# Deformable convolution: three accumulating joins per tile instead of four, with ScalarE weighting one neighbour into PSUM

## The chip, the cores and the metric

The kernel runs on one core of a Trainium2 chip as a single program. The metric is the time of one execution on the device in microseconds (us), and lower is better. Six executions of the kernel before lie between 6318.02 and 6331.94 us, with a median of 6324.73 us. The profile is that of one further execution.

## The reference

The reference is a network of four layers, each with a convolution part and a feed-forward part on a float32 image batch `x` of shape 4 x 128 x 64 x 64 (batch, channels, rows, columns). Only the second convolution part is touched here. It is a modulated deformable 3 x 3 convolution, cut to what matters:

```python
off  = conv2d(x, w_off, b_off).reshape(B, 9, 2, H, W)   # a shift per tap and pixel
mask = sigmoid(conv2d(x, w_mod, b_mod))
py, px = row + ky + dy, column + kx + dx                # where tap k looks
y0, x0 = floor(py), floor(px); wy, wx = py - y0, px - x0
sampled = v00*(1-wy)*(1-wx) + v01*(1-wy)*wx + v10*wy*(1-wx) + v11*wy*wx
sampled = sampled * mask
out = einsum('bckhw,ock->bohw', sampled, weight) + bias
```

For every pixel and each of the nine taps, four neighbouring pixels (all 128 channels) are read at a place that depends on the data, each is multiplied by a weight of its own, and the four are added. The sum then goes through a 128 x 128 matrix per tap, and the nine results are added.

## The kernel before

The whole batch stays in on-chip memory (SBUF) as `xs`, with channels on the 128 partitions. Seven phases follow each other. The second one, `recurrence_and_deformable`, ends with `deformable`, which is the stage of this document.

**Tiling.** There are four batch images. An image has 4096 pixels, in eight chunks of 512, and a chunk has four tiles of 128 pixels. Seven of the nine taps (`BY_ASK`) are sampled by gathering; the other two (`HATS`) are computed without a gather, by the generator `hats`. A step of the main loop handles one gathered tap and two tiles of a chunk, so a chunk has 7 x 2 = 14 steps, an image 112, and the stage 448.

**One step.** `taken` (L964) takes a buffer `g` out of a ring of eight (`GATHERED`), and issues two indirect DMAs on GpSimd's queue (L969), one per tile. Each brings, for each of 128 pixels, the four neighbours with 128 channels each, from a table in device memory. Then one VectorE multiplication (L977) weights all 2 x 4 x 128 values per partition, in place. The weights come from `near_w`, a copy of this chunk's weights in PSUM (the memory that TensorE accumulates in).

**The joins.** `joined` (L980) turns pixels back to channels and adds the four neighbours in one go: for each of the two tiles, four transposing matmuls against the identity (L986) accumulate into the same 128 columns of a PSUM bank `pt`. A step so has eight such matmuls. Two steps fill a bank. ScalarE copies the bank to SBUF (`turn_back`, L1092), and TensorE multiplies the copy by the tap's matrix into `po` (`convolve`, L1099), which sums over the taps. `finish` (L1107, VectorE) adds a chunk's result to `xs`.

**The order.** The order of TensorE, ScalarE, VectorE and GpSimd is the written one (`manual_schedule`); each engine runs its instructions in that order and stops at the first one that must wait. `step` (L1109) runs what earlier steps have put off: the joins of a step are issued one step after its gathers, the copy of a full bank two steps after its last join, and the tap's matmul two steps after that. Then `step` advances `side`, the preparation of the next image (`plan`: normalisation, the offset convolution, the table, the weights), and `hats` of this chunk. There is no preparation beside the last image.

**The two taps without gathering.** `hats` (L1007) has 14 parts, one per step: a transposition of small pieces into `pr` and a copy of it by ScalarE (L1046); for each of two taps a matmul into `by` (L1011) and two ScalarE functions on it (L1017, L1020); then six parts, in each of which VectorE multiplies a fresh `by` into a square (L1025, `weighted`) and, three parts later, TensorE accumulates four small matmuls from it (L1033, `sampled`). The matmul into `by` is issued one part ahead of the multiplication that reads it. The last four parts also prepare four tiles of later chunks: a matmul into `pf` (L1001) and a scaled copy by ScalarE (L1005), in `fold`. At the start of an image five `fold` stand in a row.

**PSUM.** There are eight banks: two for `pt`, one for `po` (`out`), one each for the preparation's `pd` and `pv`, one for `near_w`, and two with the tag `by`, which `pr`, `by` and `pf` share in turn.

**Keeping the weights.** At the end of `plan`, two DMAs on SyncE's queue (L955, L958) store the indices and weights of an image for a fallback that is not run on these inputs.

Of the kernel before, what the change touches and what calls it, by code (L numbers as in the profile page):

```python
# [17 lines left out]
F32 = mybir.dt.float32  # L18
# [10 lines left out]
P = 128  # L29
# [655 lines left out]
def deformable(net, sampling):  # L685
# [11 lines left out]
    Q4 = 4  # L697
    HATS, PICKED = sampling.HATS, sampling.PICKED
    NH, H0 = len(HATS), HATS[0]
    BY_ASK = [k for k in range(KK) if k not in HATS]  # L700
    BANKS = {"pt": 2, "out": 1, "pd": 1, "pv": 1, "by": 2}
    GATHERED = 8
    tables, woff, boff = sampling.tables, sampling.woff, sampling.boff
    wk, bias, grids = sampling.wk, sampling.bias, sampling.grids
    with ExitStack() as ctx:
# [173 lines left out]
        def places(b, off):  # L879
# [73 lines left out]
            made[b] = (tables[b].rearrange("y x a b c -> (y x) (a b c)"), idx, w, pieces, turns[b])  # L953
            yield
            nc.sync.dma_start(  # L955
# [5 lines left out]

        near_w = ps.tile([P, 2, Q4, KK, 4], F32, name="dcn_near_w", bufs=1)

        def taken(rows, idx, c, k, i):  # L964


            g = sb.tile([P, 2, 4 * P], F32, name="dcn_g", tag="g", bufs=GATHERED)
            for t in range(2):
                nc.gpsimd.indirect_dma_start(  # L969
                    out=g[:, t, :],  # L970
                    out_offset=None,
                    in_=rows,
                    in_offset=bass.IndirectOffsetOnAxis(ap=idx[:, Q4 * c + i + t, k : k + 1], axis=0),
                )
            near = g.rearrange("p t (q c) -> p t q c", c=P)
            by = near_w[:, c % 2, i : i + 2, k, :].unsqueeze(3).to_broadcast([P, 2, 4, P])
            nc.vector.tensor_mul(near, near, by)  # L977
            return near

        def joined(pt, i, near):  # L980

            if i == 0:
                pt[0] = ps.tile([P, CH], F32, name="dcn_pt", tag="pt", bufs=BANKS["pt"])
            for t in range(2):
                for q in range(4):
                    nc.tensor.matmul(  # L986
                        pt[0][:, (i + t) * P : (i + t + 1) * P],
                        near[:, t, q, :],
                        net.ident,
                        is_transpose=True,  # L990
                        start=i + t + q == 0,
                        stop=i + t + q == 6,
                        skip_group_check=True,
                    )
# [12 lines left out]
        def hats(b, c, po, pieces, turned):  # L1007
# [46 lines left out]
            bent(1)  # L1054
            bys.append(picked(sampling.lines[:, 0, 0, :]))
            yield
            for m, (k, p) in enumerate(todo):
                weighted(k, p)
                if m + 1 < len(todo):
                    k1, p1 = todo[m + 1]  # L1060
                    bys.append(picked(sampling.lines[:, k1, p1, :]))
                if m >= 3:
                    sampled(*todo[m - 3])
                yield
            ahead = [t for t in range(Q4 * c + 5, Q4 * c + 9) if t < NT]
            for m in range(3, 6):
                sampled(*todo[m])
                if ahead:
                    fold(b, ahead.pop(0), turned)
                yield  # L1070
            if ahead:
                fold(b, ahead.pop(0), turned)
            yield

        with tc.manual_schedule(engines=ORDERED):
# [44 lines left out]
            for b in range(B):  # L1120
# [10 lines left out]
                for c in range(NCH):  # L1131
                    nc.vector.tensor_copy(near_w[:, c % 2], w[:, Q4 * c : Q4 * c + Q4])
                    po = {}
                    busy.append(hats(b, c, po, pieces, turned))
                    if b == 0 and c < B:
                        nc.sync.dma_start(sampling.kept[c].rearrange("c p t -> p c t"), as_chunks(net.xs[:, c, :]))
                    for k in BY_ASK:
                        pt = {}
                        for i in range(0, 4, 2):
                            at(2, joined, pt, i, taken(rows, idx, c, k, i))  # L1140
                            if i:
# [1441 lines left out]
```

## Time and profile before

| what | value |
| --- | --- |
| median of six executions | 6324.73 us (6318.02 to 6331.94) |
| the profiled execution | 6331.66 us |
| its span, first to last instruction | 6329.8 us |
| mean granted TensorE clock | 0.958 |
| TensorE (PE) busy | 5794.9 us, 92% of the span |
| VectorE (DVE) busy | 4352.0 us, 69% |
| ScalarE (ACT) busy | 3404.9 us, 54% |
| GpSimd (POOL) busy | 2066.4 us, 33% |
| stage: first gather to last join | 1318.6 to 2659.9 us |
| gathers L969 | 896, 949 ns each |
| weighting L977 | 448, 1214 ns each |
| joins L986 | 3584 |

A row of a group reads: line, engine, operation, output<-inputs, sizes, count | busy us, mean ns of one | idle time of the engine just before these instructions, and what ended it. "issue" is waiting for nothing that the profile shows. PE is TensorE's matmul side and PEld its loading of weights, which overlaps with it. Starts of matmuls are recorded, but their ends are modelled, so the distance from start to start says more than a duration. A row of the timeline reads: start, duration, engine, line, operation, names, count, and in brackets the idle time before it with what ended it. In a table of windows the clock that the throttle granted to TensorE stands behind the busy times.

### The profile page before, as it was taken

The numbers are of one execution on the slowest core, as the hardware profiler recorded it, in microseconds if no ns is written. First come the engines' busy times: TensorE is split into PE (matmuls) and PEld (weight loads), VectorE is DVE, ScalarE is ACT, GpSimd is POOL, SyncE is SP. The second block draws the span as 40 slices with busy tenths as digits, with TensorE's granted clock in tenths as the row PEclk, the third lists the DMA queues.
The fourth block names the chain that finished last, engine by engine and source line by source line (L and its number), as shares of the span: only waits on it lengthen the run. The fifth ranks groups of instructions, "written<-read, shape, count | busy, mean of one in ns | idle before, by whom it ended". The sixth has DMA issues, their size and how long they took to land. (4 is left out here: it accounts for less than half of the span.)

```text
span 6329.8 us, 97956 instructions
## 1 busy us (share of the span) xinstructions
PE 5794.9 (92%) x39923; PEld 2293.1 (36%) x39923; DVE 4352.0 (69%) x4707; ACT 3404.9 (54%) x4256; POOL 2066.4 (33%) x2015
## 2 busy tenths in 40 slices
PE   8999999879898887788988999999999999999799
PEld 2222222446566666533333222222222222222233
DVE  6888887445656564446545778777777778887666
ACT  4444443322222222251154888888888888999521
POOL 4888984046666666500000111111111111111000
PEclk9999999989999999889989999999999999999899
DMA  6443340177676776651164566656665666666300
GB/s 212 87 94 82 75 94 20 47 185 217 197 212 192 207 206 183 181 190 49 41 218 144 124 144 143 137 124 140 141 140 123 141 143 138 130 130 130 76 24 27
DMA packets 291041, 836.40 MB, mean 132 GB/s; under 512 B 43356, under 2 KB 117596, under 8 KB 244492
## 3 DMA queue, kind: packets, MB, share of 16 engines
q0 software_dynamic: 109568, 505.75, 33.9%
q1 hardware_dynamic: 181004, 324.17, 17.8%
q8 instruction: 321, 5.26, 0.3%
q14 instruction: 148, 1.21, 0.1%
HBM read 416.71 MB, written 111.10 MB: 83 GB/s over the span
## 5 line engine op out<-in xcount | busy, mean ns | idle before, releaser
L1989 ACT ACTIVATE att_ex<-att_sc,att_shift 128x1024 f32<-128x1024 f32 x2048 | 2155.6, 1111 | 330.8 <-PE att_sc L1985 150.5
L2020 DVE TENSOR_TENSOR att_dve<-att_dve,att_ex 128x2048 f32<-128x2048 f32 x704 | 1634.2, 2321 | 351.1 <-ACT att_ex L1989 328.2
L1985 PE MATMUL att_sc<-att_q,att_k 32*128 32x512 f32 x8192 | 1286.5, 646 | 16.3 <-ACT att_ex L1989 16.3
L2001 PE MATMUL att_pv<-att_ex,att_vals 128*32 128x512 f32 x8192 | 1099.2, 608 | 6.6 <-ACT att_hidden L2027 5.6
L969 POOL DMA_INDIRECT dcn_g<-dcn_table,dcn_idx x896 | 850.3, 949 | 558.6 <-issue 208.0
L412 DVE SCALAR_TENSOR_TENSOR inv_prod<-inv_pk,bspan,inv_seen 128x512 f32<-128x512 f32 (+1 forms) x1120 | 774.6, 743 | 141.5 <-PE inv_pk L399 141.2
L410 POOL TENSOR_TENSOR inv_prod<-inv_seen,inv_prod 128x512 f32<-128x512 f32 (+1 forms) x672 | 837.6, 1274 | 95.4 <-ACT inv_prod L409 95.4
L2018 POOL DMA_DIRECT2D att_dma<-att_ex x224 | 192.5, 860 | 1916.7 <-ACT att_ex L1989 1669.8
L409 ACT ACTIVATE inv_prod<-inv_pk,bspan 128x512 f32<-128x512 f32 (+1 forms) x672 | 436.1, 682 | 505.1 <-PE inv_pk L399 494.0
L1985 PEld LDWEIGHTS att_sc<-att_q,att_k 32*128 32x128 f32 x8192 | 423.5, 184 | 663.8 <-issue 437.9
L977 DVE TENSOR_TENSOR dcn_g<-dcn_g,dcn_near_w 128x1024 f32<-128x1024 f32 x448 | 533.0, 1214 | 56.9 <-DMA dcn_g<-dcn_table,dcn_idx 53.2
L986 PE MATMUL dcn_pt<-ident,dcn_g 128*128 128x128 f32 x3584 | 504.1, 286 | 69.5 <-issue 28.9
L986 PEld LDWEIGHTS dcn_pt<-ident,dcn_g 128*128 128x128 f32 x3584 | 442.6, 148 | 257.6 <-issue 188.0
L399 PE MATMUL inv_pk<-inv_red,wtap 32*96 32x512 f32 (+1 forms) x3584 | 512.2, 637 | 7.3 <-DVE wtap L377 7.3
L421 PE MATMUL inv_out<-inv_prod,inv_fold 96*32 96x512 f32 (+1 forms) x3584 | 478.5, 605 | 8.5 <-DVE xs L429 8.5
L2001 PEld LDWEIGHTS att_pv<-att_ex,att_vals 128*32 128x32 f32 x8192 | 161.8, 108 | 796.6 <-issue 760.2
L1025 DVE TENSOR_TENSOR dcn_square<-dcn_hx,dcn_by 128x512 f32<-128x512 f32 x192 | 131.1, 683 | 372.7 <-remote 97.9
L1092 ACT COPY dcn_st<-dcn_pt 128x512 f32<-128x512 f32 x224 | 129.5, 579 | 372.1 <-remote 153.3
L399 PEld LDWEIGHTS inv_pk<-inv_red,wtap 32*96 32x96 f32 (+1 forms) x3584 | 131.8, 170 | 386.7 <-DVE inv_prod L412 362.7
L1099 PE MATMUL dcn_out<-dcn_st,dcn_wk 128*128 128x512 f32 x448 | 253.6, 650 | 14.2 <-issue 6.1
L1005 ACT ACTIVATE dcn_fold<-dcn_pf,dcn_turn 128x256 f32<-128x256 f32 x128 | 60.0, 473 | 354.1 <-PE dcn_pf L1001 154.6
L1033 PE MATMUL dcn_out<-dcn_square,dcn_fold 128*128 128x128 f32 x1504 | 220.1, 288 | 16.9 <-issue 15.7
(433 smaller groups left out, 5443.5 us busy)
## 6 DMA issues: line engine op xcount, KB each, us to landing
att_dma<-att_ex POOLq DMA_DIRECT2D x224, 1024.0 KB
inv_seen<-inv_image SPq DMA_DIRECT2D x256, 266.0 KB
moe_w<-in_L_ffn_weight SPq DMA_DIRECT2D x64, 1024.0 KB
dcn_table<-dcn_xt SPq DMA_DIRECT2D x64, 512.0 KB
att_dma<-att_ex SPq DMA_DIRECT2D x32, 1024.0 KB
att_dve<-att_dma POOLq DMA_DIRECT2D x32, 1024.0 KB
moe_table<-moe_xt SPq DMA_DIRECT2D x64, 288.0 KB
dcn_g<-dcn_table,dcn_idx POOLq DMA_INDIRECT x896
```

The costliest lines, as they stand in the source:

```text
L399: nc.tensor.matmul(pk[0:m], wtap[half][rg, i, blk], red[rg, h * CH : (h + 1) * CH], start=True, stop=True)
L409: nc.scalar.activation(prod[0:m, h], pk[0:m], AF.Identity, bias=by)
L410: nc.gpsimd.tensor_mul(of, view, of)
L412: nc.vector.scalar_tensor_tensor(out=of, in0=as_shape(pk[0:m], of), scalar=by, in1=view, op0=ALU.add, op1=ALU.mult)
L421: nc.tensor.matmul(po[CR * blk : CR * (blk + 1), h, :], fold[0:m], prod[0:m, h, :], start=unit == 0, stop=unit == UNITS - 1,)
L969: nc.gpsimd.indirect_dma_start(out=g[:, t, :], out_offset=None, in_=rows, in_offset=bass.IndirectOffsetOnAxis(ap=idx[:, Q4 * c + i + t, k ...
L977: nc.vector.tensor_mul(near, near, by)
L986: nc.tensor.matmul(pt[0][:, (i + t) * P : (i + t + 1) * P], near[:, t, q, :], net.ident, is_transpose=True, start=i + t + q == 0, stop=i + ...
L1985: nc.tensor.matmul(pes[h // 2][:, h % 2, :], ks[r, t * P : (t + 1) * P], q[r], start=True, stop=True)
L1989: nc.scalar.activation(ex[:, 2 * two : 2 * two + 2, :], pes[two], AF.Exp, bias=shifts[g][:, two : two + 1],)
L2001: nc.tensor.matmul(block["pv"][r], vals[:, t, r], ex[:, h, :], start=t == 0, stop=t == NT - 1)
L2020: nc.vector.tensor_add(block[who], block[who], ex)
```

## The change

In `taken`, the multiplication by VectorE leaves the first neighbour out: it covers 2 x 3 x 128 values instead of 2 x 4 x 128. The first neighbour is weighted by ScalarE, with one instruction per tile, into a new PSUM tile `first`. VectorE then adds `first` to the second neighbour. `joined` transposes and accumulates only neighbours 1 to 3, so a step has six such matmuls.

`first` takes a PSUM bank. It comes from the tag `by`, which has one bank instead of two. `hats` is rewritten for that: the matmul into `by` is issued in the same part as the multiplication that reads it, the accumulation from a square comes two parts later instead of three, and the last four parts each do one `fold`. The DMAs that keep the weights are issued while the third chunk of the image itself is sampled, instead of at the end of its preparation.

```diff
-    BANKS = {"pt": 2, "out": 1, "pd": 1, "pv": 1, "by": 2}
+    BANKS = {"pt": 2, "out": 1, "pd": 1, "pv": 1, "by": 1}
...
             made[b] = (tables[b].rearrange("y x a b c -> (y x) (a b c)"), idx, w, pieces, turns[b])
-            yield
+
+        def keep(b, idx, w):
+
             nc.sync.dma_start(
                 sampling.all_idx[b].rearrange("c p j -> p c j"), idx.rearrange("p (c t) k -> p c (t k)", c=NCH)
             )
...
         near_w = ps.tile([P, 2, Q4, KK, 4], F32, name="dcn_near_w", bufs=1)
+        first = ps.tile([P, 2, P], F32, name="dcn_first", bufs=1)
...
-            by = near_w[:, c % 2, i : i + 2, k, :].unsqueeze(3).to_broadcast([P, 2, 4, P])
-            nc.vector.tensor_mul(near, near, by)
+            for t in range(2):
+                nc.scalar.activation(
+                    first[:, t, :], near[:, t, 0, :], AF.Copy, scale=w[:, Q4 * c + i + t, k, 0:1]
+                )
+            by = near_w[:, c % 2, i : i + 2, k, 1:].unsqueeze(3).to_broadcast([P, 2, 3, P])
+            nc.vector.tensor_mul(near[:, :, 1:], near[:, :, 1:], by)
+            nc.vector.tensor_add(near[:, :, 1], near[:, :, 1], first)
             return near
...
-                for q in range(4):
+                for q in range(1, 4):
...
-                        start=i + t + q == 0,
+                        start=i + t + q == 1,
                         stop=i + t + q == 6,
...
-            bys.append(picked(sampling.lines[:, 0, 0, :]))
             yield
             for m, (k, p) in enumerate(todo):
+                bys.append(picked(sampling.lines[:, k, p, :]))
                 weighted(k, p)
-                if m + 1 < len(todo):
-                    k1, p1 = todo[m + 1]
-                    bys.append(picked(sampling.lines[:, k1, p1, :]))
-                if m >= 3:
-                    sampled(*todo[m - 3])
+                if m >= 2:
+                    sampled(*todo[m - 2])
                 yield
             ahead = [t for t in range(Q4 * c + 5, Q4 * c + 9) if t < NT]
-            for m in range(3, 6):
-                sampled(*todo[m])
+            for m in range(4, 8):
+                if m < len(todo):
+                    sampled(*todo[m])
                 if ahead:
                     fold(b, ahead.pop(0), turned)
                 yield
-            if ahead:
-                fold(b, ahead.pop(0), turned)
-            yield
...
                     busy.append(hats(b, c, po, pieces, turned))
+                    if c == 2:
+                        keep(b, idx, w)
...
-                            at(2, joined, pt, i, taken(rows, idx, c, k, i))
+                            at(2, joined, pt, i, taken(rows, idx, w, c, k, i))
```

More of the change, by code (lines that the diff above doesn't have):

```diff
@@ L962, in deformable, with taken @@
         near_w = ps.tile([P, 2, Q4, KK, 4], F32, name="dcn_near_w", bufs=1)
-        def taken(rows, idx, c, k, i):
+        first = ps.tile([P, 2, P], F32, name="dcn_first", bufs=1)
+        def taken(rows, idx, w, c, k, i):
             g = sb.tile([P, 2, 4 * P], F32, name="dcn_g", tag="g", bufs=GATHERED)
```

## The prediction, made before the changed kernel was run

> **What bounds the kernel now.** Only the stage around `taken` changes, so I read that stage alone: first the page's groups for its costs, then a table of windows for its pace, then the timeline for what a step waits for. The chain that ended last lies in the last phase and says nothing here.
>
> From the page of the kernel before, the groups that are edited, and those that share a resource with them:
>
> ```profile
> L969 POOL DMA_INDIRECT dcn_g<-dcn_table,dcn_idx x896 | 850.3, 949 | 558.6 <-issue 208.0
> ...
> L977 DVE TENSOR_TENSOR dcn_g<-dcn_g,dcn_near_w 128x1024 f32<-128x1024 f32 x448 | 533.0, 1214 | 56.9 <-DMA dcn_g<-dcn_table,dcn_idx 53.2
> L986 PE MATMUL dcn_pt<-ident,dcn_g 128*128 128x128 f32 x3584 | 504.1, 286 | 69.5 <-issue 28.9
> L986 PEld LDWEIGHTS dcn_pt<-ident,dcn_g 128*128 128x128 f32 x3584 | 442.6, 148 | 257.6 <-issue 188.0
> ...
> L1025 DVE TENSOR_TENSOR dcn_square<-dcn_hx,dcn_by 128x512 f32<-128x512 f32 x192 | 131.1, 683 | 372.7 <-remote 97.9
> ...
> L1005 ACT ACTIVATE dcn_fold<-dcn_pf,dcn_turn 128x256 f32<-128x256 f32 x128 | 60.0, 473 | 354.1 <-PE dcn_pf L1001 154.6
> ```
>
> The joins are TensorE's largest group of the stage. The other two rows to notice are the last: VectorE sits idle 372.7 us before 192 multiplications of `hats`, and ScalarE 354.1 us before 128 copies of `fold`. Both wait for TensorE.
>
> The windows of the stage, first counting the joins alone, then all work; one window for each image:
>
> ```profile
> core 0: us, PE busy (x) PEld busy (x), PEclk, DMA share, GB/s
> ...
> 2008.00:2341.00 333.00, 121.27 (x894) 106.58 (x895) 0.94 0.70 203
> 2341.00:2625.00 284.00, 116.19 (x789) 101.21 (x786) 0.90 0.64 181
> ```
>
> ```profile
> core 0: us, PE busy (x) PEld busy (x) DVE busy (x) ACT busy (x) POOL busy (x), PEclk, DMA share, GB/s
> ...
> 2008.00:2341.00 333.00, 288.62 (x1812) 207.83 (x1812) 203.63 (x250) 90.08 (x168) 210.83 (x224) 0.94 0.70 203
> 2341.00:2625.00 284.00, 227.37 (x1361) 175.21 (x1358) 147.20 (x154) 60.45 (x110) 183.91 (x195) 0.90 0.64 181
> ```
>
> A chunk has 112 joins, so the third image takes 333 / (894/112) = 41.7 us per chunk and the last, with no preparation beside it, 284 / (789/112) = 40.3. PE is busy 36.2 and 32.3 us of these. So 3.9 us less PE work in a chunk made it only 1.4 us shorter, a share of 0.36. PE is the busiest engine by far, but its work alone does not set the pace.
>
> From the timeline, a stretch in which PE waits for nothing, and one in which others wait for it:
>
> ```profile
> 1905.47 1.04 PE L986 MATMUL dcn_pt<-ident,dcn_g 128*128 128x128 f32 x8
> ...
> 1906.35 1.06 PE L1033 MATMUL dcn_out<-dcn_square,dcn_fold 128*128 128x128 f32 x8
> ```
>
> ```profile
> 2426.34 0.38 PE L1011 MATMUL dcn_by<-dcn_rowt,dcn_lines 128*128 128x512 bf16 x1
> ...
> 2429.86 0.38 PE L1011 MATMUL dcn_by<-dcn_rowt,dcn_lines 128*128 128x512 bf16 x1 [1.41 <-ACT dcn_hx L1017]
> ...
> 2432.79 0.69 DVE L1025 TENSOR_TENSOR dcn_square<-dcn_hx,dcn_by 128x512 f32<-128x512 f32 x1 [11.79 <-PE dcn_pt L986]
> ...
> 2435.68 0.95 POOL L969 DMA_INDIRECT dcn_g<-dcn_table,dcn_idx  x1 [0.30 <-issue]
> 2436.93 0.94 POOL L969 DMA_INDIRECT dcn_g<-dcn_table,dcn_idx  x1 [0.30 <-issue]
> ```
>
> Eight joins follow each other in 0.88 us, 0.11 us each. The `by` begun at 2426.34 was read only at 2432.79, by an engine idle for 11.79 us: TensorE's results reach their readers up to some 6 us after the modelled end. And gathers can't come closer than 1.25 us.
>
> **The change part by part.** All sums are made against the profiled execution: span 6329.8 us, 6331.66 us with what lies around it, 6.9 us above the median of 6324.73.
>
> *Joins removed.* 448 steps x 2 = 896 matmuls with their loads. The low price of one is its distance in the dense stretch, 0.11 us: 99 us. The high one is the mean load, 148 ns: 133 us. Since the results arrive late, PE's true pace is slower than its recorded starts; I take 133. What of it shortens the stage lies between the share 0.36 (48 us) and all (133 us). I take 0.36, since it was measured on this loop: **-48 us**.
>
> *VectorE.* From 1024 elements in 1214 ns (L977) and 512 in 683 ns (L1025, which also reads PSUM) an element costs 1.04 ns and an instruction 152 ns. The shorter multiplication is 949 ns, the added addition of 256 elements 418 ns: 1.37 us per step instead of 1.21, 69 us in all. It lies beside PE: in the third image VectorE is busy 203.63 of 333 us, and this makes it some 220. If the cover is gone, it costs up to 69 us, in the parts where VectorE has a square to make too (0.95 + 0.42 + 0.69 = 2.06 us against a step of 41.7 / 14 = 2.98).
>
> *ScalarE.* 896 new instructions of 128 elements. Below stands the 64x128 copy L802 at 298 ns, above L1005 with its scale at 473 ns. I take 350: 314 us, 0.70 us per step. ScalarE is busy 90.08 of 333 us, and will be about 170. That is hidden by PE as well. But these instructions wait for the gather and, since `first` is a single tile, for the addition of the step before. Behind them in ScalarE's order stand the copies of `pt` (L1092), of `pr`, and of `fold`, and TensorE waits for all of these. The circle addition, two weightings, addition takes 0.42 + 0.70 us and two hand-overs of some 0.05 (in the timeline PE starts 0.05 us after the ScalarE function that it waited for), 1.2 us against 2.98. So I cost it at nothing; the cover is the eight buffers, a step's data lying ready before it is wanted. The gather frees its buffer later only where the joins do.
>
> *One bank for `by`.* Per chunk eleven uses now wait for the reader of the use before: the second of the first two matmuls, six multiplications, four `fold`, less the first that had to wait anyway. Between two uses PE has six joins (0.66 us), half a tap's matmul and, in most parts, four small ones (0.88 us); the reader needs 0.47 to 0.69 us and two hand-overs. Low end: nothing. High end: the whole reader exposed, 0.8 us x 11 x 32 = 282 us. By the table of PE's waits in the stage it waits today 12.2 us for squares, 5.1 for the functions and 6.3 for `fold` at these places, 23.6 us with two banks. The value is nearer to this low row than to the high end, and I add half as much again: **+12 us**. A gain is possible too: the fifth and sixth square now wait for `sampled` matmuls issued just before them, to get their buffer, and with a lag of two they won't; a few us, not counted.
>
> *Five `fold` in a row*, once per image: with one bank each pays its matmul (0.40 us in the row of L1001) beside its copy instead of under it, 4 x 5 x 0.40 = **+8 us**.
>
> *Keeping the weights later.* Eight DMAs of 144 or 576 KB move within SyncE's queue past nothing else in its order of the changed program. The first gather of the stage waited for one of them last (80.5 us, but the table ended beside it): between 0 and 2 us less, taken as 0.
>
> Sum: -48 + 12 + 8 = -28 us, 6303.7 us for such an execution, **6297 us** as the median.
>
> A row speaks against even this: the clock. It was 0.94 with preparation beside the image and 0.90 without, where PE is busy 80% and not 87% of the time. Less PE work may lower it everywhere.
>
> The Trainium skill, page "TensorE: Matmul & The Clock Gate", part 1, says that about one idle window of 3.4 us is enough to bring the array to half its clock; by that rule, with the first three images at the last one's 0.90, the 882 us that PE is busy in them, less 75 to 100 removed, would grow by 3 to 4%, some 30 us by estimate, and the whole gain be gone.
>
> I keep the measured share, which already holds the lower clock of the last image.
>
> **The rivals.**
>
> *TensorE is the bound.* For it: results come late, as a backlog in TensorE would make them. Then all 99 to 133 us count, less 8: 6200 to 6234 us. GpSimd allows it: 896 x 1.25 = 1120 us against a stage of 1341. Against it: the share of 0.36.
>
> *Slower: PE stands at the single bank.* Place: the eleven uses per chunk. Mechanism: a late result reaches VectorE or ScalarE, which now answers in the same part; ScalarE's weighting of the next step and VectorE's addition queue behind that answer, and TensorE waits for all three. For it: VectorE idles 372.7 / 192 = 1.9 us before each square, ScalarE 354.1 / 128 = 2.8 us before each copy. Against it: much of that idling is running ahead. Price: 0.13 us per use and chunk (47 us / 352) is where it decides against a gain of 48 less 8; at 0.25 us it is 88 - 40 = +48, about 6373 us, and at 0.35 us 6408.
>
> *Nothing.* PE's time turns into idling: the gain falls to the 20 us that the one bank and `fold` cost, 6312 to 6337 us. For it: the 1.25 us of the gathers are 35 of 41.7 us per chunk.
>
> **How the numbers follow.** Chances: forecast 0.40 (own range 6265 to 6312), TensorE as the bound 0.13, nothing 0.10, slower 0.37. A time within 0.2% of 6324.73 (6312 to 6337) can't be told from no change. So faster 0.53, same 0.10, slower 0.37. The range reaches from inside the second case to most of the slower one: 6215 to 6400.
>
> **What would show it.** 2688 joins; VectorE's two instructions near 950 and 420 ns; ScalarE's near 350 ns, with busy time about 700 us in the stage; a chunk of the third image near 40.8 us. Waits of PE's `by` and `pf` for squares and `fold` near 36 us: above 90 us in sum, the slower case is true. A clock of 0.90 or less with a chunk as before would show the idle case. Wrong it would be above all if a join costs its full time or if ScalarE's order holds up `pt`.

## The result, and the profile after

The changed kernel takes **6343.13 us** (median of 22 runs, 6329.92 to 6358.55), the kernel before beside it 6326.49 us (46 runs). The ratio is 1.0028 with a 95% interval of 1.0021 to 1.0034: slower by 0.28%, some 17 us. The profiled execution took 6347.88 us, its span is 6346.1 us and its mean clock 0.956, against 6331.66, 6329.8 and 0.958 before.

The groups of the page of the kernel after (`first` is L980, the multiplication L984, the addition L985, the joins L994, `by` L1019, squares L1033, `pf` L1009):

```profile
L972 POOL DMA_INDIRECT dcn_g<-dcn_table,dcn_idx x896 | 850.0, 949 | 578.0 <-issue 200.7
...
L980 ACT ACTIVATE dcn_first<-dcn_g,dcn_w 128x128 f32<-128x128 f32 x896 | 330.7, 369 | 385.1 <-DVE dcn_g L985 248.2
...
L994 PE MATMUL dcn_pt<-ident,dcn_g 128*128 128x128 f32 x2688 | 406.9, 292 | 81.3 <-issue 31.8
...
L984 DVE TENSOR_TENSOR dcn_g<-dcn_g,dcn_near_w 128x768 f32<-128x768 f32 x448 | 424.1, 947 | 9.0 <-DMA dcn_g<-dcn_table,dcn_idx 7.3
...
L985 DVE TENSOR_TENSOR dcn_g<-dcn_g,dcn_first 128x256 f32<-128x256 f32 x448 | 188.8, 421 | 328.0 <-ACT dcn_first L980 209.6
```

The change did what its diff says: 2688 joins, 896 instructions more on ScalarE, VectorE's work in two pieces. New is the idle time before the addition, 328.0 us, 209.6 of it for ScalarE's product; and ScalarE in turn stands 248.2 us for the addition. Neither engine is the busiest of the stage.

The windows that cover the stage, first gather to last join, of the kernel before and of the kernel after:

```profile
core 0: us, PE busy (x) PEld busy (x) DVE busy (x) ACT busy (x) POOL busy (x), PEclk, DMA share, GB/s
1318.60:2660.20 1341.60, 1137.66 (x6973) 826.93 (x6974) 767.06 (x915) 337.61 (x625) 850.33 (x896) 0.92 0.69 197
```

```profile
core 0: us, PE busy (x) PEld busy (x) DVE busy (x) ACT busy (x) POOL busy (x), PEclk, DMA share, GB/s
1326.10:2688.00 1361.90, 1070.39 (x6084) 724.96 (x6083) 828.01 (x1363) 639.48 (x1523) 849.95 (x896) 0.91 0.68 194
```

The stage grew by 20.3 us although PE's busy time in it fell by 67.3. So PE's idle time rose from 203.9 to 291.5 us. The whole difference lies here; each of the phases around the stage agrees within 7 us, and together they are 4 us shorter.

By image, the third and the last, of the kernel after, all work and then the joins alone:

```profile
2028.00:2369.00 341.00, 278.81 (x1593) 184.52 (x1593) 215.22 (x359) 165.91 (x392) 212.27 (x224) 0.91 0.70 200
2369.00:2655.00 286.00, 206.98 (x1169) 149.33 (x1168) 160.48 (x253) 127.69 (x310) 185.54 (x197) 0.90 0.64 179
```

```profile
2028.00:2369.00 341.00, 101.04 (x672) 84.48 (x672) 0.91 0.70 200
2369.00:2655.00 286.00, 91.15 (x594) 74.88 (x594) 0.90 0.64 179
```

A chunk now has 84 joins: 341 / (672/84) = 42.6 us in the third image and 286 / (594/84) = 40.4 in the last, after 41.7 and 40.3 before. The clock of the third image fell from 0.94 to 0.91.

PE's waits in the stage of the kernel after (sum, times, longest, in us):

```profile
PE dcn_by L1019 <- issue: 45.5, 35, 5.6
PE dcn_pt L994 <- issue: 31.8, 54, 2.4
PE dcn_pt L994 <- DVE dcn_g L985: 28.4, 22, 5.7
PE dcn_pf L1009 <- issue: 23.6, 18, 2.1
PE dcn_by L1019 <- DVE dcn_square L1033: 23.3, 16, 4.2
PE dcn_out L1102 <- DVE xs L1110: 21.2, 14, 1.7
PE dcn_pf L1009 <- ACT dcn_fold L1013: 17.8, 17, 3.1
...
PE dcn_pt L994 <- ACT dcn_st L1095: 12.3, 20, 0.9
...
PE dcn_by L1019 <- ACT dcn_hx L1025: 7.2, 4, 2.3
```

And what answered to them in the kernel before:

```profile
PE dcn_by L1011 <- issue: 20.8, 17, 2.6
PE dcn_pt L986 <- ACT dcn_st L1092: 20.0, 17, 2.4
...
PE dcn_by L1011 <- DVE dcn_square L1025: 12.2, 6, 4.2
PE dcn_pt L986 <- DVE dcn_g L977: 11.1, 3, 9.3
...
PE dcn_pf L1001 <- ACT dcn_fold L1005: 6.3, 2, 5.0
...
PE dcn_out L1099 <- DVE xs L1107: 5.3, 5, 1.6
PE dcn_by L1011 <- ACT dcn_hx L1017: 5.1, 3, 2.1
```

Three places grew: the single bank (`by` and `pf`, most of it idle time without a named releaser), the joins' wait for VectorE's result, from 11.1 to 28.4 us, and the wait of a chunk's first matmul into `po` for `finish`, which reads the chunk before, from 5.3 to 21.2 us. The wait that the prediction feared from ScalarE's order, `pt` for `st`, is small: 12.3 us, after 20.0 before.

### The profile page after: what moved, and what is told of

The parts are those of the page before. It is cut to its first block, busy times and chain, and to the rows that moved or that the text cites. A ratio compares the mean times of both kernels' runs of the same rounds, so it can differ in the third digit from the quotient of the medians.

```text
span 6346.1 us, 98629 instructions
## 1 busy us (share of the span) xinstructions
PE 5727.6 (90%) x39027; PEld 2192.7 (35%) x39027; DVE 4413.1 (70%) x5155; ACT 3705.4 (58%) x5152; POOL 2066.0 (33%) x2015
## 5 line engine op out<-in xcount | busy, mean ns | idle before, releaser
L1990 PE MATMUL att_sc<-att_q,att_k 32*128 32x512 f32 x8192 | 1281.3, 643 | 16.3 <-ACT att_ex L1994 16.3
L980 ACT ACTIVATE dcn_first<-dcn_g,dcn_w 128x128 f32<-128x128 f32 x896 | 330.7, 369 | 385.1 <-DVE dcn_g L985 248.2
L994 PE MATMUL dcn_pt<-ident,dcn_g 128*128 128x128 f32 x2688 | 406.9, 292 | 81.3 <-issue 31.8
L994 PEld LDWEIGHTS dcn_pt<-ident,dcn_g 128*128 128x128 f32 x2688 | 337.5, 151 | 292.0 <-issue 178.2
L984 DVE TENSOR_TENSOR dcn_g<-dcn_g,dcn_near_w 128x768 f32<-128x768 f32 x448 | 424.1, 947 | 9.0 <-DMA dcn_g<-dcn_table,dcn_idx 7.3
L985 DVE TENSOR_TENSOR dcn_g<-dcn_g,dcn_first 128x256 f32<-128x256 f32 x448 | 188.8, 421 | 328.0 <-ACT dcn_first L980 209.6
L1102 PE MATMUL dcn_out<-dcn_st,dcn_wk 128*128 128x512 f32 x448 | 266.6, 681 | 46.1 <-DVE xs L1110 21.2
L1033 DVE TENSOR_TENSOR dcn_square<-dcn_hx,dcn_by 128x512 f32<-128x512 f32 x192 | 130.6, 680 | 165.8 <-PE dcn_by L1019 61.3
L2492 PE MATMUL top_po<-top_xg,top_we 128*128 128x512 f32 x512 | 233.2, 598 | 0.0
```

The source lines that it names most:

```text
L984: nc.vector.tensor_mul(near[:, :, 1:], near[:, :, 1:], by)
L994: nc.tensor.matmul(pt[0][:, (i + t) * P : (i + t + 1) * P], near[:, t, q, :], net.ident, is_transpose=True, start=i + t + q == 1, stop=i + ...
L1990: nc.tensor.matmul(pes[h // 2][:, h % 2, :], ks[r, t * P : (t + 1) * P], q[r], start=True, stop=True)
```

## The experiments

The runs came in several batches, each on one chip, and these are of two kinds: in some the kernel before takes 6323 to 6336 us, as in the prediction, in others 6129 to 6131. The difference lies in this stage alone (the last section shows it). Every ratio is against the kernel before in the same batch, in brackets its 95% interval; microseconds are differences of the medians. I call the kinds the 6330 chip and the 6130 chip. The name goes further than the record: the chip of two batches has the number 12 there, and the kernel before took 6128.70 us in one and 6322.97 us in the other. Whether that was one and the same chip is not on record.

### One part at a time, on a 6330 chip

**One bank.** The kernel before with the single `by` bank and the rewritten `hats`, four joins, nothing new on ScalarE:

```diff
-    BANKS = {"pt": 2, "out": 1, "pd": 1, "pv": 1, "by": 2}
+    BANKS = {"pt": 2, "out": 1, "pd": 1, "pv": 1, "by": 1}
...
-            bys.append(picked(sampling.lines[:, 0, 0, :]))
             yield
             for m, (k, p) in enumerate(todo):
+                bys.append(picked(sampling.lines[:, k, p, :]))
                 weighted(k, p)
...
```

> The kernel before with one bank for `by` and the rewritten `hats` alone: four joins, VectorE's full multiplication, nothing on ScalarE. Bank theory (the single bank ate the gain): slower by 40 to 90 us, PE's waits for squares and folds above 50 us. Circle theory (ScalarE and VectorE wait for each other through the single tile `first`, and hold TensorE): within 15 us of before. Idle theory (the joins were never on the path): within 15 us too.

Measured: 6354.81 against 6336.27 us, 1.0028 [1.0019, 1.0037], +18.5 us. PE's waits in its stage:

```profile
PE dcn_by L1011 <- issue: 66.0, 31, 7.4
PE dcn_by L1011 <- DVE dcn_square L1025: 39.0, 18, 5.0
PE dcn_pf L1001 <- ACT dcn_fold L1005: 30.3, 18, 7.1
...
PE dcn_by L1011 <- ACT dcn_hx L1017: 13.6, 7, 4.4
```

These four sum to 148.9 us, against 44.4 in the kernel before (20.8 + 12.2 + 6.3 + 5.1). The bank with its new `hats` costs what the prediction took for it with `fold` (+20), but that is only about a sixth of the 104.5 us by which these waits grew; the rest replaces idling that PE had elsewhere. PE's wait for `finish`, 16.6 us here, also comes with this part of the change.

**Joins alone.** The first neighbour is left out of the sum, VectorE still multiplies all four:

```diff
-                for q in range(4):
+                for q in range(1, 4):
...
-                        start=i + t + q == 0,
+                        start=i + t + q == 1,
...
```

> The kernel before with the first neighbour left out of the joins and nothing in its place (one of four terms of each sampled value is missing): 896 joins fewer, all else as it was. Prediction's term: 48 us faster; if TensorE is the bound, 99 to 133 us faster. Idle theory: within 15 us of before. Bank and circle theories: at least 40 us faster, since both say that the gain was there and was eaten.

Measured: 0.9979 [0.9969, 0.9990], -13.7 us instead of -48. The window over its stage:

```profile
core 0: us, PE busy (x) PEld busy (x) DVE busy (x) ACT busy (x) POOL busy (x), PEclk, DMA share, GB/s
1319.70:2654.90 1335.20, 1064.61 (x6046) 737.46 (x6078) 766.73 (x915) 337.03 (x625) 851.27 (x896) 0.90 0.67 198
```

PE has 73.1 us less to do and the stage is 6.4 us shorter in this execution: PE's idle time rose by 66.7 us. The clock fell from 0.92 to 0.90. By estimate, PE's work at full clock would be 1137.66 x 0.92 = 1047 us before and 1064.61 x 0.90 = 958 here. The 89 us between them are 96 at an unchanged 0.92, or 0.107 us per join, near the 0.11 read from the dense stretch; PE's busy time fell by 73, so the lower clock took back some 23 (12 to 35, since the clocks are rounded to two places; 32 of the 6078 matmuls here also have no record, which makes PE's busy time a few us too small).

**ScalarE in place, two banks.** Three joins; ScalarE weights the first neighbour in the gathered buffer, VectorE adds it. The old bank and `hats`:

```diff
+            for t in range(2):
+                nc.scalar.activation(
+                    near[:, t, 0, :], near[:, t, 0, :], AF.Copy, scale=w[:, Q4 * c + i + t, k, 0:1]
+                )
...
+            nc.vector.tensor_add(near[:, :, 1], near[:, :, 1], near[:, :, 0])
...
```

> Three joins, ScalarE weights the first neighbour in place in the gathered buffer, VectorE adds it from there; two banks for `by` and the old `hats`, no tile `first`. Bank theory: the gain of the joins comes through, 30 to 60 us faster than before. Circle theory: the circle through the single tile is gone as well, so faster too, by the same. Order theory (ScalarE's order, in which the weightings wait for gathers and for nothing else now, still holds up the copies of `pt`): no gain, 0 to 20 us slower. Idle theory: within 15 us of before.

Measured: 1.0004 [0.9995, 1.0014], +4.8 us: 18.5 us above the joins alone.

**VectorE alone, two banks.** Three joins; the old multiplication by all four weights, then the addition; ScalarE has no part:

```diff
             nc.vector.tensor_mul(near, near, by)
+            nc.vector.tensor_add(near[:, :, 1], near[:, :, 1], near[:, :, 0])
...
```

> Three joins, VectorE alone weights all four neighbours and adds the first to the second (1214 + about 420 ns per step, 188 us more VectorE work); ScalarE, the banks and `hats` as before. Order and circle theories: ScalarE is not involved, so 20 to 50 us faster than before unless VectorE becomes the bound. Bank theory: the same. Idle theory: 0 to 30 us slower.

Measured: 0.9986 [0.9977, 0.9995], -8.3 us, faster than the kernels before and after, and 5.4 us above the joins alone; the intervals of these two overlap. So the addition's 188 us on VectorE cost next to nothing here, and handing a quarter of the multiplication to ScalarE as well, which frees 119 us of VectorE (543 to 424), costs 13 us more than keeping it. PE's wait for VectorE's result, with ScalarE in place and then with VectorE alone:

```profile
PE dcn_pt L991 <- DVE dcn_g L982: 81.2, 46, 9.3
```

```profile
PE dcn_pt L987 <- DVE dcn_g L978: 19.4, 9, 9.8
```

The shorter instructions deliver later. In the first of the two kernels, VectorE waited for ScalarE:

```profile
DVE dcn_g L982 <- ACT dcn_g L977: 264.2, 116, 8.8
```

The parts on this chip: joins 0.9979, bank 1.0028, the weighting with its addition 1.0004 / 0.9979 = 1.0025. Their product is 1.0032; the changed kernel's 1.0028 [1.0021, 1.0034] fits. It used another tile for the product, so the third factor is that of a near relative. That the parts multiply like this is not shown: one bank with three joins and no weighting would test it, and that ran on 6130 chips alone (below).

### The same on 6130 chips

**One bank with three joins**, no weighting of the first neighbour, which is left out:

> One bank and the rewritten `hats`, and three joins with the first neighbour left out (one of four terms of each sampled value is missing); nothing on ScalarE. The bank alone cost 0.28%, the joins alone gave 0.21%. If the two lie on the same path one after the other, their sum: 5 us slower than before (0.0 to 0.15%). If TensorE now stands at the bank for as long as the joins took, the joins give nothing here: 18 us slower, as with the bank alone.

0.9985 [0.9976, 0.9993], -7.6 us. **The rewritten `hats` with two banks**, four joins:

```diff
             yield
             for m, (k, p) in enumerate(todo):
+                bys.append(picked(sampling.lines[:, k, p, :]))
                 weighted(k, p)
...
-                if m >= 3:
-                    sampled(*todo[m - 3])
+                if m >= 2:
+                    sampled(*todo[m - 2])
...
```

> The rewritten `hats` with two banks, four joins. If the bank itself costs (a reader's answer exposed at each use): back to within 6 us of before. If the rewriting costs (the multiplication now reads a `by` of its own part, so that a late result holds VectorE at once): some 18 us slower, as with one bank.

1.0019 [1.0010, 1.0027], +12.3 us with no bank taken away. So on this chip the rewritten order costs something by itself; how it splits from the bank on the 6330 chip was not tried. One bank with three joins lies 19.8 us below it, so here the joins are worth at least that unless the bank itself is a gain, more than the 13.7 us on the 6330 chip with the old `hats`: what a part gives depends on what stands beside it.

**No reading of `by`.** In the kernel before, the square is made from `hxs[k]` twice; the matmul into `by` is issued and no square reads it. Then the same with three joins:

```diff
-                nc.vector.tensor_mul(sq, hxs[k], by)
+                nc.vector.tensor_mul(sq, hxs[k], hxs[k])
```

> The kernel before, with the square made from ScalarE's function alone instead of its product with `by` (the output's two ungathered taps are wrong); the matmul into `by` is still made, but nobody waits for it and it waits for nobody. Handshake theory (VectorE held at the squares until TensorE's late result sets the pace, the joins hide behind it): 30 to 100 us faster. Gather theory (GpSimd's 1.25 us per gather and its ring set the pace): within 15 us of before. Pace theory (TensorE is slower than its recorded starts and is the bound): within 15 us too.

> As the run before, and three joins with the first neighbour left out. Handshake theory: with the hold gone the joins come onto the path, 50 to 130 us faster than the run before. Gather theory: 0 to 15 us faster than the run before. Pace theory: 99 to 133 us faster than the run before.

1.0034 [1.0021, 1.0048] and 1.0026 [1.0014, 1.0037]. A wait less made the kernel slower, so these two say nothing on the price of the hand-over. What did change is GpSimd:

```profile
L969 POOL DMA_INDIRECT dcn_g<-dcn_table,dcn_idx x896 | 879.9, 982 | 354.3 <-issue 150.8
```

Its gathers take 982 ns instead of the 948 to 954 of kernels in which the squares and the weighting read their second operand from PSUM. That this makes the 21 us is not shown.

**The changed kernel again, and its relatives**, on one such chip: as it is; with two halves of the bank for `first` in turn; without weighting; and weighting in place beside one bank.

```diff
-        first = ps.tile([P, 2, P], F32, name="dcn_first", bufs=1)
+        firsts = ps.tile([P, 2, 2, P], F32, name="dcn_first", bufs=1)
+        turn_of = [0]
...
+            first = firsts[:, turn_of[0] % 2]
+            turn_of[0] += 1
```

> The changed kernel as it is, beside its parts and relatives. Two chips have shown two speeds of the stage so far: about 6330 us for the kernel before, where TensorE's results reach their readers late, and 6129 us, where gathers follow each other at 1.25 us. Theory 'sum of parts' (a dear bank, +0.28%, a small gain of the joins, -0.21%, a dear weighting, +0.25%): 1.0025 to 1.0035 where the kernel before takes about 6330. Rival 'gathers set the pace': where it takes about 6130, 0.999 to 1.001, since TensorE and the other engines have room beside 28 x 1.25 = 35 us per chunk.

> The changed kernel, with two halves of the same bank taken in turn for first, so that the weighting of a step waits for the addition two steps back and not for that of the step before. Theory 'circle' (the single tile ties ScalarE's weightings to VectorE's additions one by one, and what stands behind them in ScalarE's order comes late): VectorE's wait for ScalarE at the addition falls from 210 us to below 120 and the time by 0.15% or more against the changed kernel beside it. Theory 'place' (a step's weighting is late because it stands behind waits for TensorE in ScalarE's order, whatever its buffer): within 0.1% of the changed kernel, the wait above 170 us.

> The kernel before with one bank for by, the rewritten hats and three joins; the first neighbour is left out of the sum, and nothing weights it. On a chip like the first: theory 'sum of parts' gives +0.28% - 0.21% = 1.0007, theory 'together' (with the joins gone the bank costs less, as 0.9985 beside 1.0019 for the hats alone showed on the other chip) 0.997 to 0.999. What the changed kernel takes above this one is the price of its weighting: 0.2% by the first theory, 0.4% by the second.

> The changed kernel's division of work with one difference: ScalarE weights the first neighbour in its place in the gathered buffer instead of into the PSUM tile first; one bank for by, rewritten hats, and the weights kept where they were. Each step's weighting has its own buffer, so it never waits for an addition. Theory 'circle': faster than the changed kernel by 0.15% or more, near the sum with the ring. Theory 'sum of parts': 1.0004 + 0.28% = 1.0032, as the changed kernel or slightly above.

| kernel | ratio | us |
| --- | --- | --- |
| the changed kernel | 1.0023 [1.0014, 1.0032] | +16.3 |
| two halves for `first` | 1.0020 [1.0010, 1.0030] | +14.8 |
| one bank, three joins, no weighting | 0.9984 [0.9975, 0.9993] | -8.9 |
| weighting in place, one bank | 1.0021 [1.0012, 1.0030] | +15.7 |

The rival in which the gathers hide it all is wrong: the change costs as much here. The theory of a circle over the single `first` falls too, but by the last row alone. The second half did not loosen the circle: in all 447 pairs of steps the next weighting starts only after the addition ahead of it has ended, as with the single tile, and ScalarE waits as long for VectorE. The changed kernel, then the one with two halves:

```profile
ACT dcn_first L980 <- DVE dcn_g L985: 275.6, 196, 3.6
```

```profile
ACT dcn_first L983 <- DVE dcn_g L988: 279.7, 200, 4.7
```

The two halves are parts of one tile in one bank, and something still orders them; what does is not shown. With the weighting in place 221 of the 447 start before that addition has ended, so there the circle is open, and the kernel is no faster (+15.7 for +16.3). The weighting as a whole costs 25.2 us above the same kernel without it. Where the room goes is seen in VectorE's waits for gathers, without weighting and in the changed kernel:

```profile
DVE dcn_g L977 <- DMA dcn_g<-dcn_table,dcn_idx: 169.0, 146, 5.2
```

```profile
DVE dcn_g L985 <- ACT dcn_first L980: 165.4, 138, 5.8
DVE dcn_g L984 <- DMA dcn_g<-dcn_table,dcn_idx: 51.4, 51, 5.2
```

Without weighting VectorE stands ready for 169.0 us before the gathers land, and the stage is 1132.0 us by its window, hardly more than 896 x 1.25 = 1120 us of gathers. In the changed kernel it waits for ScalarE instead, and the stage takes 1157.3.

### What makes the weighting dear

Two theories: the hand-over in VectorE's order (its addition stands for a product behind ScalarE's waits for TensorE), or the work itself. These four ran on a 6330 chip (6322.97 us for the kernel before). **Unread:** VectorE adds the unweighted neighbour, and ScalarE's product is never read. **Late:** two halves for `first`, and the addition of a step (`added`) just ahead of the next step's multiplication; then the same in place with two banks and the old `hats`. **VectorE alone** with two banks once more, on this chip. The first diff is of the unread kernel, the second of the late one:

```diff
-            nc.vector.tensor_add(near[:, :, 1], near[:, :, 1], first)
+            nc.vector.tensor_add(near[:, :, 1], near[:, :, 1], near[:, :, 0])
```

```diff
+            added()
             by = near_w[:, c % 2, i : i + 2, k, 1:].unsqueeze(3).to_broadcast([P, 2, 3, P])
             nc.vector.tensor_mul(near[:, :, 1:], near[:, :, 1:], by)
-            nc.vector.tensor_add(near[:, :, 1], near[:, :, 1], first)
+            owed.append((near, first))
...
```

> The changed kernel, but VectorE adds the unweighted first neighbour from the gathered buffer; ScalarE's product in first is written and never read. So all instructions and their work stay, and only the hand-over from ScalarE to VectorE is gone. Theory 'hand-over' (VectorE stands at the addition for a weighting that waits behind ScalarE's waits for TensorE, 165 us in the profile on a chip that takes 6129 us for the kernel before): near the kernel without weighting, 0.998 to 1.000 there, and at least 0.2% less than the changed kernel on a slower chip. Theory 'work' (69 us more on VectorE, 330 us more on ScalarE, gathered buffers read by two engines): 1.001 to 1.0025, as the changed kernel.

> The changed kernel with two halves of the bank for first, and VectorE's addition of a step put off until just before the multiplication of the next step; the joins stand where they stood. Work and hand-over stay, but a weighting has a step's time, about 2.6 us, before it is waited for. Theory 'hand-over': VectorE's wait for ScalarE falls from 165 us below 60, ratio 0.998 to 1.0005 where the kernel before takes about 6129. Theory 'work': 1.0015 to 1.003. If the wait falls and the time does not, the addition waits instead of standing, and TensorE waits for it a step later.

> The kernel before with its two banks and its hats, three joins, ScalarE weighting the first neighbour in place, and VectorE's addition put off until just before the multiplication of the next step. Theory 'hand-over': 0.997 to 0.999, faster than both kernels and than VectorE alone, since the bank's price is gone too. Theory 'work': 0.9995 to 1.0015.

> The kernel before with three joins, where VectorE weights all four neighbours and adds the first to the second; ScalarE does nothing new, two banks, the hats of before. On the first chip it gave 0.9986. Theory 'hand-over': VectorE waits for nobody and has room (0.42 us more in a step of 2.6), so 0.998 to 1.000 here too. Theory 'work': VectorE gets 188 us more, more than in the changed kernel, so it is at least as dear as the changed kernel's 1.0023.

| kernel | ratio | us |
| --- | --- | --- |
| unread | 1.0100 [1.0084, 1.0115] | +61.0 |
| late, one bank | 1.0313 [1.0299, 1.0327] | +198.7 |
| late, in place, two banks | 1.0013 [1.0004, 1.0022] | +7.4 |
| VectorE alone, two banks | 0.9983 [0.9974, 0.9992] | -9.0 |

The first two miss both theories, and the late kernel did not do what it was written for. GpSimd's waits in the unread kernel point to why taking the hand-over away did not help:

```profile
POOL dcn_g L972 <- issue: 292.2, 597, 4.0
POOL dcn_g L972 <- ACT dcn_st L1095: 55.3, 38, 2.9
POOL dcn_g L972 <- ACT dcn_fold L1013: 34.0, 22, 2.2
POOL dcn_g L972 <- ACT dcn_first L980: 33.2, 40, 2.7
```

In the changed kernel no gather is listed as waiting for ScalarE. Here three rows give 122.5 us: TensorE no longer waits for ScalarE's reading, ScalarE falls behind, and the buffer is free only when it has read it. I read this as a wait that was taken from one engine and given to another. The late kernel's longest waits:

```profile
DVE dcn_g L973 <- ACT dcn_first L990: 500.1, 213, 9.1
...
POOL dcn_g L980 <- PE dcn_pt L1006: 319.5, 209, 5.3
PE dcn_pt L1006 <- DVE dcn_g L973: 274.1, 221, 9.6
```

The wait rose to 500.1 us instead of falling below 60. The timeline shows what is waited for. The addition in the last row is that of the step whose product was ready at 2102.12, and it starts 0.03 us after the product of the next step:

```profile
2101.34 0.78 ACT L990 ACTIVATE dcn_first<-dcn_g,dcn_w 128x128 f32<-128x128 f32 x2
...
2112.11 0.77 ACT L990 ACTIVATE dcn_first<-dcn_g,dcn_w 128x128 f32<-128x128 f32 x2
...
2112.91 0.42 DVE L973 TENSOR_TENSOR dcn_g<-dcn_g,dcn_first 128x256 f32<-128x256 f32 x1 [9.12 <-ACT dcn_first L990]
```

That holds for all 447 additions that have a next step: none starts before the next step's weighting has ended. The two halves are tied here as well, so the move made an addition wait for a later product, where it was to give it more time; PE waits 274.1 us for VectorE, and the buffers come free late. In place, where each step has its own buffer, 271 of 447 additions start before the next weighting has ended, and that kernel lies 7.4 us above the kernel before. It also has two banks and the old `hats`, so how the 198.7 us split between the tie and the bank stays open. In that kernel the hand-over did get a step's time, and VectorE still waits 217.9 us for ScalarE (264.2 with the addition at its old place, on another chip): most of the lateness is in ScalarE's own order. It lies 16.4 us above VectorE alone beside it.

VectorE alone repeated its gain. The last pair, both with three joins, asks whether that also holds beside one bank, and ran on a 6130 chip: VectorE alone with one bank and the rewritten `hats`, and once more the kernel without weighting.

```diff
-    BANKS = {"pt": 2, "out": 1, "pd": 1, "pv": 1, "by": 2}
+    BANKS = {"pt": 2, "out": 1, "pd": 1, "pv": 1, "by": 1}
...
             nc.vector.tensor_mul(near, near, by)
+            nc.vector.tensor_add(near[:, :, 1], near[:, :, 1], near[:, :, 0])
```

> One bank for by, rewritten hats and three joins, as in the changed kernel, but VectorE weights all four neighbours and adds the first to the second; ScalarE has no part in a step. Theory 'ScalarE in the loop' (a step's buffer passes through ScalarE's order, in which it stands behind copies that wait for TensorE): 0.2% or more below the changed kernel, 0.9985 to 1.0005 on either kind of chip, within 0.1% of the sum without weighting. Rival 'VectorE's work' (its second instruction comes in the way of the squares and of finish, which TensorE waits for): as the changed kernel, 1.002 to 1.0035, since VectorE has still more to do than there.

> The same with no weighting of the first neighbour, which is left out of the sum. On a chip that takes about 6129 us for the kernel before it gave 0.9985 and 0.9984. On one that takes about 6325: by the sum of the parts measured there (one bank +0.28%, joins -0.21%) 1.0007; if the bank costs less once the joins are gone, 0.997 to 0.999.

1.0018 [1.0009, 1.0027], +8.7 us, and 0.9991 [0.9981, 1.0000], -8.3 us. There VectorE's work alone costs 17 us. The weighting with ScalarE cost 25.2 us in the batch before, but 1.0018, 1.0020, 1.0021 and 1.0023 for the four ways to weight can't be told apart. VectorE's wait for the gathers in the kernel of VectorE alone, then in that without weighting beside it:

```profile
DVE dcn_g L977 <- DMA dcn_g<-dcn_table,dcn_idx: 65.0, 63, 6.1
```

```profile
DVE dcn_g L977 <- DMA dcn_g<-dcn_table,dcn_idx: 167.1, 139, 5.8
```

The slack ahead of VectorE is spent here too, as in the changed kernel. So the rival 'VectorE's work' holds on the 6130 chip with one bank; on the 6330 chip with two banks 'ScalarE in the loop' does. What stays open is the 6330 chip with one bank, with VectorE alone and without weighting, and the 6130 chip with two banks. Which of the two makes the weighting dear in the changed kernel on the 6330 chip is therefore not shown.

## Why the prediction was wrong

It summed -48 for the joins, +20 for the bank and nothing for ScalarE and VectorE, -28 us. Measured one at a time on a 6330 chip these are -14, +18.5 and +18.5, which add up to +23; the change itself gave +17. Two steps failed: the gain from the joins, and the cover over ScalarE and VectorE.

- **The joins, -48 us: the term that failed by most.** Alone they gave -13.7 us (-20 to -6 by the interval). Both factors were too high: PE's time fell by 73 us, not 133, and of that 0.19 by the medians (0.09 in the profiled execution) came out, not 0.36. The low price of 0.11 us per join was the nearer one (0.107 at an unchanged clock). The share came from comparing the third image with the last; but the last lacks its preparation on VectorE, ScalarE and the DMA queues too, so the 1.4 us could not be put down to PE alone. The share was nearer to an upper bound than to a value. Why so little of PE's saved time comes out is only partly shown: the clock took some of it, and PE's idle time, which rose by 66.7 us, the rest.
- **The clock, named and not counted.** It fell to 0.91 over the stage, and from 0.94 to 0.91 in the third image. The Trainium skill, page "TensorE: Matmul & The Clock Gate", part 1, says that about one idle window of 3.4 us brings the array to half its clock; beside it the prediction estimated that the whole gain might go. With the joins alone the lower clock took back some 23 us of 96 by estimate, so the direction agrees, but most of the loss is PE's idle time and not its pace. That single windows of idling lowered the clock is not shown here.
- **ScalarE hidden, cost nothing: failed.** The size was right (369 ns for 350; 639 us busy in the stage, where 700 was written). The cover was not: weighting in place with the addition costs 18.5 us above the joins alone on the 6330 chip with two banks, 13 us more than VectorE alone. The prediction named the circle over the single `first` and `pt` behind ScalarE's order as the ways in which this could break. The circle is there, but opening it gave nothing (in place, 6130 chip), and PE's wait for `st` fell from 20.0 to 12.3 us. What the changed kernel shows in their place is VectorE's addition waiting for ScalarE, 209.6 us, and PE for VectorE, 28.4 us for 11.1. That this hand-over makes the price is shown with two banks on the 6330 chip alone.
- **VectorE, 949 and 418 ns, hidden.** Measured 947 and 421. With VectorE alone the addition was all but hidden on the 6330 chip with two banks (5.4 of 188 us, not resolved); on the 6130 chip with one bank 17 us show.
- **One bank +12 and five `fold` +8: right in size, partly by luck.** 18.5 us together. The prediction took the growth of PE's waits as the price; with the bank alone these waits grew by 104.5 us, and about a sixth of that came out as time. The signs were waits of 48.3 us at squares, functions and `fold` (23.3 + 7.2 + 17.8) for some 36, well under the 90 of the slower case. But idle time without a releaser at the same matmuls rose from some 22 to 69.1 us (45.5 + 23.6), and the sign left that out.
- **Keeping the weights, 0.** Not tried by itself; the kernel that weights in place kept the old order of these DMAs and can't be told from the changed one.
- **The rivals.** TensorE as the bound falls: 67 us less of its work, and the stage longer. The slower case gave the sign but not the size or the deciding mechanism: the bank costs 18.5 / 352 = 0.05 us per use. By the prediction's own terms it needed (48 - 8) / 352 = 0.11 to turn the gain into a loss; the 47 us behind its 0.13 are a slip. The bank counted only because the joins gave 14 and not 48, and the weighting took more than that again. 'Nothing', PE's time turning into idling, is the nearest in mechanism: the idle time rose by 88 us.

## What to carry to other kernels

Before work is taken from the busiest engine, measure what taking it away gives: one run that leaves the work out shows what the gain is worth in place, here 14 us where the change had 37 us of costs of its own. When work is split between engines, count the hand-over and not the busy time alone: an engine that is idle half of the time, but stands behind others' waits in a written order, delivers late, and with two banks the engine with the longer instruction was the better place. A wait taken away goes to whoever stood behind it, so look at buffers and at how far each engine may run ahead before a wait is removed. And check in the trace that an experiment did what it was written for: two halves of a tile looked like two buffers in the code and were none in the timeline.

## What the hardware showed beside this

**Two kinds of chip.** The changed kernel's stage is 1361.9 us on a 6330 chip and 1157.3 on a 6130 chip, while the rest of the program takes 4984.2 and 4985.9 us. On the 6130 chip the changed kernel's PE is busy 1004.8 us in the stage at a clock of 0.95, against 1070.39 at 0.91. There the timeline (the kernel with the rewritten `hats` and two banks) shows a result read at once:

```profile
2102.24 0.39 PE L1011 MATMUL dcn_by<-dcn_rowt,dcn_cols 128*128 128x512 bf16 x1
...
2102.67 0.69 ACT L1017 ACTIVATE dcn_hx<-dcn_by,dcn_steps 128x512 f32<-128x512 f32 x1 [1.76 <-PE dcn_by L1011]
```

The reader, idle for 1.76 us, starts 0.04 us after the modelled end, where on the 6330 chip the prediction showed one that came 6 us late. So the late results that looked like a backlog in TensorE seem to go with the kind of chip; these two rows are of different kernels, and what makes results late was not found. A price measured on one kind need not hold on the other.

**GpSimd and VectorE.** A gather's instruction took 948 to 954 ns where VectorE's second operands came from PSUM, 956 to 969 in the seven kernels with the addition from the gathered buffer, and 982 to 984 with squares from SBUF alone. The Trainium skill, page "GPSIMD Engine Reference", section "1. Specifications", says that GpSimd shares its interfaces to SBUF with VectorE and that VectorE's instructions with two SBUF inputs contend with it; the direction agrees with these rows.

**Two banks, three joins, VectorE alone** is the best version with the whole sum that ran on a 6330 chip: 0.9986 and 0.9983 in two batches, faster than the kernels before and after.
